# Layer 1's experts computed by columns, with a block's expert copied to a fixed tile, and whole batches stored at once

## The chip, the cores and the metric

The kernel runs on one core of a Trainium2 chip. The metric is the device time of one launch in microseconds, measured as the median of several runs. A profiled execution gives, beside its own time, a trace of every instruction on TensorE (PE, with its weight loads PEld), VectorE (DVE), ScalarE (ACT), GpSimd (POOL) and SyncE (SP).

## The reference

Four layers act on x [4, 256, 256] (batch, tokens, features) with a context [4, 512, 128], all in fp32. Each layer adds a cross-attention of the normalised x to x, and then a feed-forward of the normalised x:

```python
x = x + L0_xattn(ln(x), ctx);  x = x + L0_ffn(ln(x))   # routed low-rank adapters
x = x + L1_xattn(ln(x), ctx);  x = x + L1_ffn(ln(x))   # mixture of experts
x = x + L2_xattn(ln(x), ctx);  x = x + L2_ffn(ln(x))   # one of two experts
x = x + L3_xattn(ln(x), ctx);  x = x + L3_ffn(ln(x))   # 64 chosen tokens a batch

def L1_ffn(h):                      # E = 8 experts, top 2, F = 176, FS = 352
    scores = softmax(h @ gate.T)
    w, idx = top_k(scores, 2);  w = w / (sum(w) + 1e-20)
    cw = scatter(w, idx)                                # [tokens, E]
    g = silu(einsum('th,efh->tef', h, w_gate)) * einsum('th,efh->tef', h, w_up)
    y = einsum('te,teh->th', cw, einsum('tef,ehf->teh', g, w_down))
    return y + swiglu(h, sw_gate, sw_up, sw_down)       # the shared expert, FS wide
```

The layers 1 to 3 have 16 heads of 128 in their cross-attention, and this is where most of the time goes. The change is in `L1_ffn` and in how x is loaded at the beginning and stored at the end.

## The kernel before

The main function is `bounded_path`. x stays in SBUF for the whole kernel, one tile `x_sb[b]` of [128, 2, 256] for each batch: 128 partitions, two chunks of 128 tokens, 256 features. Behind `bounded_path` a register `again` is loaded from a word `over`, and a second, general path would run if it were set (it is not). That is line 2856 for the load and line 2859 for the branch, and each of the five engines does both.

The order of instructions on PE, ACT, DVE and POOL is the order in which the program writes them (`tc.manual_schedule`), so an instruction that waits holds up everything that its engine has after it. SP's order, with most of the loads and stores, is left to the framework. PSUM banks come from `bank(tag, ...)`: tag `s` has four, `mm` two, `o` and `t` one each. A tile with `bufs=n` is reused after n allocations. A matmul of fp32 appears in the trace as two records.

**Layer 1's FFN** lies between 583.9 and 709.4 us, and has two kinds of matmul work that are woven together.

*The shared expert* is class `Shared`, one object for each of 8 chunks of 128 tokens (two a batch). `rise` has the tokens as stationary operand and the weights (352 columns of `wgu`) as moving one: 4 matmuls, 8 records, into two `s` banks (L2131). ACT takes silu of one (L2136), DVE multiplies by the other (L2137). The result has tokens on partitions, so `turn` transposes it in three pieces (L2143), and ACT copies these to SBUF (L2145, L2146). `fall` has three matmuls with the down weights into the `o` bank (L2152), and DVE adds that bank to x (L2156).

*The routed experts* are class `Block`: 23 blocks of 128 slots. A slot holds one token of one expert, and a block belongs to one expert only. `gather` fetches the 128 tokens by an indirect DMA from POOL (L2267). `turn_in` transposes them (pxg, L2275), and ACT copies them to `xgT`. `rise` loads the number of the block's expert from `ebi` into a register of PE (L2281), multiplies the tokens by a slice of `wgu` that the register addresses, 2 × 176 columns (pgu, L2287), then silu on ACT (L2292), and on DVE the product with the slot's weight `wslot` (L2294). `turn` transposes that product in two pieces (pgT, L2300, L2301), and DVE copies them to `gT` (L2303, L2304). `fall` multiplies with the expert's down weights, 128 rows and then 48 rows of it (pyr, L2309, L2312), into the `o` bank; ACT copies the bank to `yr` (L2316), and SP writes it to `yd` in DRAM. Later class `Back` gathers from `yd` the two rows of each token, and DVE adds them to x.

Between these two stands the routing. `chosen` works out the two experts of each token (on DVE and ACT). `ranks`, `lists`, `listed` and `indices` work out which token goes to which slot, with long chains of small DVE operations; `ranks` has six matmuls on PE ahead of its chain (L2166 to L2168), and `listed` has 32 records on PE (plist, L2236) that take what DVE makes in L2235. The order, written out by hand, is

```python
ranks(); shared[2].turn(); shared[3].rise(); shared[2].fall(); lists()
shared[3].turn(); shared[4].rise(); listed(range(2 * N8)); indices(); shared[3].fall()
```

Then the blocks run as a pipeline of four steps: in turn j the loop does `turn_in` of block j + 2, `rise` of block j + 1, `turn` of block j and `fall` of block j − 1. Four gathers are issued ahead. After the loop the next layer's weights are folded (pm, L985, and n_sb, L1004) between the last two chunks of the shared expert.

The weights of this FFN are loaded during layer 1's attention of batch 0: `load_waiting` issues one waiting DMA for each of eight pairs of heads.

**The end.** `put` (L2769) adds the chosen tokens' FFN output to x: one matmul for each batch and chunk (L2775), a DVE addition (L2777), and a store of 128 tokens, 128 KB (L2781), on SP or on ACT's queue. `x` is loaded and stored with token c × 128 + p at partition p, chunk c, so a run of one partition is 1 KB.

## Time and profile before

| | |
|---|---|
| three runs | 1482.56, 1485.49, 1488.65 us (median 1485.49) |
| profiled execution | 1485.29 us, of which the span of its trace is 1483.6 us |
| granted TensorE clock | 0.993 of full, mean over the span |
| layer 1's FFN | 583.9 to 709.4 us |
| its blocks, first pxg to last pyr | 618.9 to 684.6 us |
| POOL's gathers of the blocks (L2267) | 23, 22.0 us busy |
| the DVE chain of `ranks` | 597.7 to 601.0 us |
| register load of `ebi` on PE (L2281) | 23, 0.30 us each |
| last two stores issued by SP and by ACT | 1474.5 to 1476.6 us, 1475.0 to 1476.6 us |

Busy times are by engine and count an instruction from its start to its end; for PE the ends are modelled, and consecutive matmuls overlap, so PE's pace is read from the starts or from the chain of waits. A trace comes from one execution. The chain of waits is the work that ended last, followed back from the last instruction.

### The profile page before, as it was taken

To read this page: it belongs to the slowest core of one execution; us is meant where nothing else is said; L and a number is where in the kernel's file an instruction comes from. 1 tells how busy PE (TensorE), PEld (TensorE's weight loads), DVE (VectorE), ACT (ScalarE), POOL (GpSimd) and SP (SyncE) were. 2 spreads that over 40 slices of the span, in tenths; PEclk is the share of its full clock that TensorE was granted. 3 is DMA by queue.
4 is the path that set the end of the run, shared out by engine and by line. 5 is a ranking of instruction groups with operands and counts; after the bars stand their busy time and mean duration, and the time that the engine had idled before them with its cause. 6 is when DMAs were issued, how large, how long until landed. Compare 5 with 4: busy or idle time off the path is not lost.

```text
span 1483.6 us, 19771 instructions
## 1 busy us (share of the span) xinstructions
PE 1442.5 (97%) x7311; PEld 937.3 (63%) x7311; DVE 898.1 (61%) x1946; ACT 573.2 (39%) x1100; POOL 665.4 (45%) x779
## 2 busy tenths in 40 slices
PE   8999999999999999999999999999999999999997
PEld 7665667566556666656556666666885566666666
DVE  5666783575676566423675656547345666767684
ACT  4666453433433333234443333333224433333331
POOL 2221332566665454231466655556003665455560
PEclk9999999999999999999999999999999999999998
DMA  5000210210000001271210000000311000000000
GB/s 164 2 1 2 67 50 26 74 35 0 8 1 8 1 8 47 58 215 48 61 32 8 8 1 1 1 1 0 107 36 44 18 0 1 1 0 1 1 1 31
DMA packets 40037, 43.36 MB, mean 29 GB/s; under 512 B 3898, under 2 KB 36891, under 8 KB 39933
## 3 DMA queue, kind: packets, MB, share of 16 engines
q1 hardware_dynamic: 36956, 35.85, 8.0%
q0 software_dynamic: 1872, 5.11, 1.3%
q8 instruction: 60, 0.98, 0.3%
q10 hardware_dynamic: 1104, 1.05, 0.2%
q14 instruction: 45, 0.36, 0.1%
HBM read 36.89 MB, written 5.11 MB: 28 GB/s over the span
## 4 chain that ended last, share of the span: by engine, by line
PE 88%; DVE 6%; POOL 4%; issue 2%; ACT 0%; DMA 0%; DVEq 0%; POOLq 0%; ACTq 0%
PE ps L1815 21%; PE po L1821 21%; PE paq L1785 5%; PE pao L1785 4%; PE pbq L1785 4%; PE pbo L1785 3%; PE ph L2492 2%; PE po L2529 2%; PE pgu L2287 2%; PE ps L1321 2%; PE po L1331 2%; PE pyf L1448 2%; PE paf L1398 1%; PE py L1897 1%; PE pm L985 1%
## 5 line engine op out<-in xcount | busy, mean ns | idle before, releaser
L1828 POOL TENSOR_TENSOR half<-pT 128x1024 f32<-128x1024 f32 x96 | 225.8, 2353 | 376.7 <-ACT pT L1818 326.9
L1815 PE MATMUL ps<-qT,cT 128*128 128x512 f32 x768 | 345.5, 592 | 0.0
L1821 PE MATMUL po<-pT,c_sb 128*128 128x512 f32 x768 | 345.2, 592 | 0.0
L1818 ACT ACTIVATE pT<-ps,mbias 128x512 f32<-128x512 f32 x384 | 263.6, 687 | 163.7 <-PE ps L1815 153.7
L1821 PEld LDWEIGHTS po<-pT,c_sb 128*128 128x128 f32 x768 | 145.9, 190 | 183.7 <-issue 183.7
L1815 PEld LDWEIGHTS ps<-qT,cT 128*128 128x128 f32 x768 | 138.8, 190 | 137.9 <-issue 137.3
L1825 ACT COPY oT<-po 128x512 f32<-128x512 f32 x96 | 56.2, 586 | 263.6 <-PE po L1821 263.6
L1862 POOL TENSOR_TENSOR oT<-oT,wide 128x512 f32<-128x512 f32 x90 | 116.2, 1311 | 26.2 <-DVE wide L1861 26.2
L1325 ACT ACTIVATE pT<-ps 128x512 f32<-128x512 f32 x128 | 66.1, 603 | 41.0 <-PE ps L1321 40.8
L1795 DVE TENSOR_TENSOR qT<-qT,paq 128x128 f32<-128x128 f32 x90 | 25.6, 284 | 89.8 <-ACT qT L1794 89.5
L1834 DVE TENSOR_TENSOR half<-half 128x512 f32<-128x512 f32 x96 | 72.1, 751 | 10.2 <-POOL half L1828 10.2
L1795 DVE TENSOR_TENSOR w<-w,pao 128x128 f32<-128x128 f32 x21 | 6.0, 286 | 109.4 <-ACT w L1794 109.4
L1836 DVE STREAM_TRANSPOSE turned<-half 128x512 f32<-128x512 f32 x96 | 68.3, 711 | 6.3
L1785 PEld LDWEIGHTS paq<-xnT_a,m_sb 128*128 128x128 f32 x360 | 58.0, 191 | 21.5 <-PE po L1821 10.5
L1785 PE MATMUL paq<-xnT_a,m_sb 128*128 128x128 f32 x360 | 70.7, 278 | 0.1
L1785 PE MATMUL paq<-xx,m_x 128*128 128x128 f32 x360 | 69.8, 276 | 0.0
L1840 DVE TENSOR_REDUCE sums<-turned 128x16 f32<-128x512 f32 x96 | 65.9, 686 | 3.3
L1785 PE MATMUL pao<-n_x,ox 128*128 128x128 f32 x336 | 65.2, 276 | 0.3 <-POOL ox L1711 0.3
L1861 DVE STREAM_TRANSPOSE wide<-rz 128x512 f32<-128x512 f32 x96 | 62.2, 686 | 0.1
L1794 ACT COPY qT<-paq 128x128 f32<-128x128 f32 x90 | 23.9, 265 | 85.2 <-PE paq L1785 82.8
L1798 DVE TENSOR_TENSOR qT<-qT,pbq 128x384 f32<-128x384 f32 x90 | 49.9, 554 | 9.4
L1785 PEld LDWEIGHTS paq<-xx,m_x 128*128 128x128 f32 x360 | 54.6, 192 | 0.0
(401 smaller groups left out, 2584.8 us busy)
## 6 DMA issues: line engine op xcount, KB each, us to landing
wo<-in_L_wo SPq DMA_DIRECT2D x12, 512.0 KB
wq<-in_L_wqT SPq DMA_DIRECT2D x11, 512.0 KB
yd<-yr SPq DMA_DIRECT2D x23, 128.0 KB
w<-in_F_w SPq DMA_DIRECT2D x4, 512.0 KB
wgu<-in_F_wgT SPq DMA_DIRECT2D x2, 880.0 KB
wgu<-in_F_wuT SPq DMA_DIRECT2D x2, 880.0 KB
wk<-in_L_wkT SPq DMA_DIRECT2D x11, 128.0 KB
wv<-in_L_wvT SPq DMA_DIRECT2D x11, 128.0 KB
```

The lines of the kernel that those rows point to most:

```text
L1325: nc.scalar.activation(pT[kp][:, j], ps[j], AF.Exp)
L1785: nc.tensor.matmul(p[:, at, :], lhsT=lhsT, rhs=rhs, start=(k == 0 and at == 0), stop=(k == len(of) - 1 and i == which[-1]),)
L1815: nc.tensor.matmul(ps, lhsT=cT[:, b, k * P : (k + 1) * P], rhs=qT, start=True, stop=True)
L1818: nc.scalar.activation(pT[:, k, :], ps, AF.Exp, bias=mbias[:, b, k : k + 1])
L1821: nc.tensor.matmul(po, lhsT=c_sb[:, b, k, :], rhs=pT[:, k], start=(k == 0), stop=(k == NK - 1))
L1825: done["head"] = nc.scalar.copy(raw, po).ins
L1828: nc.gpsimd.tensor_tensor(half, pT[:, 0:2], pT[:, 2:4], ALU.add)
L1834: nc.vector.tensor_tensor(part, half[:, 0], half[:, 1], ALU.add)
L1836: nc.vector.transpose(turned.rearrange("p f i -> p (f i)"), part)
L1840: nc.vector.tensor_reduce(sums[b, hp // 4][:, hp % 4, :], turned, AX.X, ALU.add)
L1861: nc.vector.transpose(wide, rzs[b, hp // 4][:, hp % 4, :, None].to_broadcast([P, NB, 32]))
L1862: eng.tensor_tensor(outs[b, hp], outs[b, hp], wide.rearrange("p f i -> p (f i)"), ALU.mult)
```

## The change

- The shared expert's object is now a whole batch. `rise(ks)` has the weights as stationary operand, 128, 128 and 96 columns of them, and 256 tokens as moving operand. The result has the hidden features on partitions and goes straight into `gT`; there is no `turn`. `fall(c)` is as before, for one chunk. The order around the routing is written anew.
- A block's expert is copied by DVE from `wr1`, a new tile of all experts' weights, to a fixed tile `we` (two buffers). The expert's number is loaded into a register of PE and of DVE. `rise` has `we` as stationary operand in three pieces (128 gate, 128 up, and 112 with the rest of both: 48 gate, 16 of zeros, 48 up), and the tokens as moving operand. Silu is in two pieces, the product also, and lands in `gT`; there is no `turn`. The slot's weight is applied by ACT on the way from the `o` bank to `yr`. The loop is one step shorter.
- `wr1` takes eight DMAs in place of four whole ones, `wgu` keeps the shared part, POOL zeroes the gap, and `load_waiting` issues two at a time.
- x has token 2p + c at partition p, chunk c: runs of 2 KB. `put` does its matmuls first, then the additions batch by batch, and stores each batch at once, 256 KB, odd ones on SP, even ones on ACT's queue. `put(0, [0])` stores nothing.
- `again` is loaded before the last `block` and `put`.

```diff
-        nc.sync.dma_start(x_sb[b], t["x"][b].rearrange("(c p) d -> p c d", p=P))
+        nc.sync.dma_start(x_sb[b], t["x"][b].rearrange("(p c) d -> p c d", c=NC))
...
+    FQ = 2 * P + 64 + FL
+    wr1 = load_fw("fa", [P, ND, NE, FQ], ...)
+    nc.gpsimd.memset(wr1[:, :, :, 2 * P + FL : 2 * P + 64], 0.0)
     wgu = load_fw(
-        "fa",
-        [P, 2, ND, FT],
+        "fs",
+        [P, 2, ND, FS],
...
-            load_waiting()
+            load_waiting(2)
...
+                def rise(self, ks):
+                    for k in ks:
                         m = min(P, FS - k * P)
+                        pp = bank("s", [P, 2, S], f"psh{self.b}_{k}")
+                        for i in range(2):
+                            for d in range(ND):
+                                nc.tensor.matmul(
+                                    pp[:m, i, :], lhsT=wgu[:, i, d, k * P : k * P + m],
+                                    rhs=xnT1[self.b][:, d, :],
+                                    start=(i == 0 and d == 0), stop=(i == 1 and d == ND - 1),
+                                )
+                        g = fp.tile([P, S], F32, tag="gs", name=f"gs{self.b}_{k}", bufs=3)
+                        nc.scalar.activation(g[:m], pp[:m, 0, :], AF.Silu)
+                        nc.vector.tensor_tensor(self.gT[:m, k, :], g[:m], pp[:m, 1, :], ALU.mult)
...
+                def weights(self):
+                    j = self.j
+                    self.e = nc.values_load(state["ebi"][0:1, j : j + 1], engines=[E.PE, E.DVE], ...)
+                    self.w = fp.tile([P, ND, FQ], F32, tag="we", name=f"we{j}")
+                    nc.vector.tensor_copy(self.w[:, :, None, :], wr1[:, :, bass.ds(self.e, 1), :])
+
                 def rise(self):
-                    e = self.e = nc.values_load(state["ebi"][0:1, j : j + 1], engines=[E.PE], ...)
-                    pp = bank("s", [P, 2, FE], f"pgu{j}")
-                    for d in range(ND):
-                        nc.tensor.matmul(
-                            pp, lhsT=self.xgT[:, d, :], rhs=wgu[:, :, d, bass.ds(e * FE, FE)],
-                            start=(d == 0), stop=(d == ND - 1),
-                        )
...
+                    pp = bank("s", [P, 3, P], f"pgu{j}")
+                    for k, m in enumerate((P, P, FQ - 2 * P)):
+                        for d in range(ND):
+                            nc.tensor.matmul(
+                                pp[:m, k, :], lhsT=self.w[:, d, k * P : k * P + m], rhs=self.xgT[:, d, :],
+                                start=(k == 0 and d == 0), stop=(k == 2 and d == ND - 1),
+                            )
+                    sg = fp.tile([P, 2, P], F32, tag="sg", name=f"sg{j}")
+                    nc.scalar.activation(sg[:, 0, :], pp[:, 0, :], AF.Silu)
+                    nc.scalar.activation(sg[64 : 64 + FL, 1, :], pp[:FL, 2, :], AF.Silu)
+                    self.gT = fp.tile([P, 2, P], F32, tag="gT", name=f"gT{j}")
+                    nc.vector.tensor_tensor(self.gT[:, 0, :], sg[:, 0, :], pp[:, 1, :], ALU.mult)
+                    nc.vector.tensor_tensor(
+                        self.gT[:FL, 1, :], sg[64 : 64 + FL, 1, :], pp[64 : 64 + FL, 2, :], ALU.mult
+                    )
...
-                    done["slots"] = nc.scalar.copy(yr, py).ins
+                    done["slots"] = nc.scalar.activation(yr, py, AF.Copy, scale=state["wslot"][:, j : j + 1]).ins
...
+            shared[0].fall(0)
             chosen(B - 1)
+            shared[1].rise([0, 1, 2])
             ranks()
+            shared[0].fall(1)
+            shared[1].fall(0)
+            shared.append(Shared(2))
+            shared[2].rise([0])
             lists()
+            shared[2].rise([1])
+            shared[1].fall(1)
             listed(range(2 * N8))
             indices()
+            shared[2].rise([2])
...
+            shared[2].fall(0)
+            shared[2].fall(1)
+            shared[3].rise([0])
-            for j in range(-2, NBLK + 2):
+            for j in range(-2, NBLK + 1):
...
+                    blocks[j + 2].weights()
                     blocks[j + 2].turn_in()
                 if 0 <= j + 1 < NBLK:
                     blocks[j + 1].rise()
                 if 0 <= j < NBLK:
-                    blocks[j].turn()
-                if 0 <= j - 1 < NBLK:
-                    blocks[j - 1].fall()
+                    blocks[j].fall()
...
+        ps = {}
         for c in chunks:
             for b in (2 * i + 1, 2 * i):
...
+        for b in (2 * i + 1, 2 * i):
+            for c in chunks:
+                xc = x_sb[b][:, c, cols]
+                nc.vector.scalar_tensor_tensor(xc, ps[b, c][:, cols], wts[:, b, c : c + 1], xc, ALU.mult, ALU.add)
+            if store:
+                (nc.sync if b % 2 else nc.scalar).dma_start(out[b].rearrange("(p c) d -> p c d", c=NC), x_sb[b])
...
+        again = nc.values_load(over[0:1, 0:1], ...)
         block(1, z)
         put(1, cols=z)
+    return again
```

## The prediction

> **What bounds the kernel now.** I read the page first: the totals and the shares of the chain that ended last.

> ```profile
> span 1483.6 us, 19771 instructions
> ...
> PE 1442.5 (97%) x7311; PEld 937.3 (63%) x7311; DVE 898.1 (61%) x1946; ACT 573.2 (39%) x1100; POOL 665.4 (45%) x779
> ...
> PE 88%; DVE 6%; POOL 4%; issue 2%; ACT 0%; DMA 0%; DVEq 0%; POOLq 0%; ACTq 0%
> ```

> TensorE is busy 97% of the span: an edit pays if it takes time from PE's stream or from PE's waits. So I read the stage of layer 1's FFN, 583.9 to 709.4 us, first by windows (columns: stretch, length, busy time of PE, PEld, DVE, ACT, POOL, granted clock, DMA share, GB/s), with the one half-clock stretch inside it:

> ```profile
> 583.90:709.40 125.50, 121.42 (x548) 79.62 (x546) 47.74 (x171) 49.60 (x137) 31.18 (x33) 0.99 0.38 112
> 609.00:612.50 3.50, 3.50 (x12) 2.85 (x12) 1.18 (x7) 0.00 (x0) 1.39 (x2) 0.51 0.00 0
> ```

> PE idles 4.1 us in 125.5; DVE works 48. Then the chain of waits in the stage (start, duration, what): it gives PE's pace by matmul width.

> ```profile
> 593.45 1.30 PE pysh L2152 x6
> 594.75 0.34 PE pgsT L2143 x3
> 598.06 2.37 PE psh L2131 x8
> ...
> 655.75 0.37 PE pxg L2275 x2
> 656.12 1.19 PE pgu L2287 x4
> 657.31 0.11 PE pgT L2300
> 657.42 0.11 PE pgT L2301
> 657.53 0.43 PE pyr L2309 x2
> 657.96 0.63 PE pyr L2312 x2
> ...
> 707.81 0.89 PE pm L985 x8
> ```

> A record (an fp32 matmul is two) costs 0.296 us at 352 columns (2.37/8), 0.217 at 256 (1.30/6), 0.111 at 128 (0.89/8). The middle six lines are one block: 2.84 us, back to back.

> **The change, part by part.** *Blocks.* PE loses the two transposes (0.22), and pgu goes from 1.19 to 12 records of 128 columns, 12 × 0.111 = 1.33. pxg and pyr keep their instructions: 0.37 + 1.33 + 1.06 = 2.76, so −0.08 a block, −1.8 for 23.

> *Shared expert.* Before, 8 chunks × (2.37 + 0.34 + 1.30) = 32.1. After, 4 batches × (24 records × 0.217 + 2 × 1.30) = 31.2: −0.9.

> *What the blocks add beside PE.* DVE loses the weighting (L2294, 0.40) and both copies, gains two mults of the copies' shapes, a register load and the weight copy of 128x736. Rows by form (line, busy, mean ns, idle before), then register loads and one SBUF-to-SBUF operation by line (min/median/max ns):

> ```profile
> L2303 DVE COPY gT<-pgT 128x128 f32<-128x128 f32 x23 | 6.5, 284 | 0.5 <-PE pgT L2301 0.5
> L1004 DVE COPY n_sb<-pn 128x512 f32<-128x512 f32 x8 | 5.4, 689 | 8.2 <-PE pn L1001 5.2 <-PE pm L985 3.0
> L2856 DVEq TENSOR_LOAD <-over x1: 542/542/542, 1474.4 to 1474.4; - x1
> L925 DVE TENSOR_SCALAR xn_f<-x_sb,mv_f,rstd_f x24: 404/1355/2166, 135.5 to 1046.0; 128x256 f32<-128x256 f32 x24
> ```

> From 284 at 128 elements to 689 at 512 is 1.05 ns an element: 736 make 0.92 us. Load, copy, mults: 0.54 + 0.92 + 0.55 = 2.0 us of DVE against 2.76 of PE: hidden, with 0.75 to spare. The dependence closes too: pgu's end, silu and mults, next copy, next pgu come to about 4 us, and the two buffers allow two blocks, 5.5. ACT has a second silu, 1.3 us a block; the slot weight rides on yr's copy. The register load on PE stays; POOL's gathers stay. Cost 0 with that cover. Without it, each 0.1 us a block beyond 2.76 is 2.3 us.

> The unknown is a DVE copy between SBUF tiles while POOL works. L925 is such a form: 0.40 us when it runs freely, 1.36 in the median, 2.17 at worst. Bounds for ours: 0.4 (it moves 2.9 times as much, so no less) and 0.92 + 1.8 (the worst hold-up) = 2.7. POOL's gather takes 0.96 us of each 2.8 (22.0 us for 23), so a copy meets one about a third of the time, and waits at most its length: 0.92 to 1.4 on average, and I take 0.92, nearest to the plain copies.

> [...]

> *The hand-written order and its waits.* What falls away or comes is read off the order of each engine. Before's idle is 4.1 us, or 4.8 with the 0.16 us by which each of some five waits is under-counted (a transpose is drawn 0.27 long and followed after 0.11). After, worked through with the rows' durations:
> - shared[1].fall(0) stands right behind shared[0].fall(1). Both use the single bank `o`. The add that frees it is queued on DVE behind ranks(), fourteen instructions and 3.3 us from prank on (597.7 to 601.0). PE ends the first fall at 599.1, the add ends at 602.2: 3.1 us idle. Everything on PE waits behind it.
> - The mult of shared[2].rise([0]) is on DVE ahead of lists(), so plist starts near 609.9: 1.6 idle, in place of 1.3.
> - fall(2,0) waits for its last mult (0.7), fall(2,1) for the add before it (0.7); the first pxg and the first pgu wait for xgT and the copy (0.6 + 0.5); fall(0,0) 0.2.
> - The loop is a step shorter: its tail has one wait for `o`, 0.6, where before had two.

> Sum 8.0. Stage: −1.8 − 0.9 + 8.0 − 4.8 = +0.5. Letting each wait end as early as its data allow gives −0.1. I take +0.3. The yd rows (SP) are read by Back's gathers with over 4 us in hand, and lose 2 of that: 0.

> *Clock.* The half-clock stretch cost 1.6 us. It follows a 1.26 us wait at 604.4; the other three of the kernel's body follow waits of 1.0, 1.7 and 2.5 us, while five waits of 1.1 to 1.9 us were followed by none. After has the same wait and a longer one: 0 to +1.7, I take +0.8. [...]

> *Loads.* 15 weight loads in place of 8 in layer 1's first batch, two per step, needed 260 us later: 0. x in runs of 2 KB instead of 1 KB: 0 to −0.3, taken −0.1.

> *End.* The last pieces, in the order of time and by line:

> ```profile
> 1474.09 1.13 DVE L2777 SCALAR_TENSOR_TENSOR x_sb<-py,wts,x_sb 128x128 f32<-128x128 f32 x4 [0.58 <-PE py L2775]
> 1474.47 2.14 SPq L2781 DMA_DIRECT2D out<-x_sb  x2
> ...
> L2859 SPq EVENT_SEMAPHORE  x8: 17/17/17, 1481.0 to 1481.5; - x8
> ...
> L2859 SPq COMPARE_BRANCH  x1: 45/45/45, 1477.3 to 1477.3; - x1
> ```

> SP issues two stores until 1476.6, loads `over` (0.53), branches, and goes on 3.7 us later, at 1481.0; then the end. After, SP has one store, after the second add (1474.7): issued by 1475.1, branch at 1475.7, on at 1479.4. ACT branches as early. The stores' data were in by 1478, so the branch still sets the end: −1.6, less 0.1 for a larger store. Bounds −0.2 (the store's 256 KB or another engine ends last) and −2.2 (the second store's long issue, 1.72, gone on both queues).

> **Sum**, against the profiled execution, 1485.29 us (span 1483.6 and 1.7 around it; the median of the runs, 1485.49, is 0.2 away): 1485.3 + 0.3 + 0.8 − 0.1 − 1.5 = **1484.8**. With the bounds of wait, clock and end: 1482 to 1488. Half a per cent, 7.4 us, is about what a measurement of this kernel can tell from no change; I forecast no change by that measure, 0.65.

> **Rivals.** *The copy paces the loop* (slower). Place: DVE's load, copy and mults, 23 times. It decides once load and copy pass 2.2 us (2.76 − 0.55). At 1.9 + 0.6 a block costs 3.05, +6.6 in all, less what the head of the loop hides: +5. At 2.7 + 0.54 it is 3.8, +24. Half held up, half not, lies between: 1490 to 1502, say 1494. [...] Against: POOL is busy 31 us of the stage's 125. Chance 0.18.

> *The small costs of the block's joints vanish* (faster). pxg takes 0.37 for 0.22 of transposes, and pyr 1.06 for 4 × 0.217 = 0.87: 0.34 a block that I keep, as it goes with the 48-row weights. If the register operations or the addressed operand pgu<-wgu cause it, 23 × 0.34 = 7.8 goes. With the bank wait partly filled and no second half clock (−0.8): 1485.3 − 7.8 − 1.5 + 0.3 = 1476.3, and 1474 to 1478. For: both stand beside addressed operands. Against: pyr's operand stays addressed. Chance 0.17.

> *The end does not move:* another engine's branch or the larger stores set it. 1486.1; inside my forecast.

> **How the numbers follow.** My own case 0.65, copy 0.18, joints 0.17. The range cuts the copy's upper part and the joints' lower: 1477 to 1491. Faster by over 0.5% is below 1478.1: the joints, 0.17. Slower, above 1492.9, is most of the copy's case and a little of mine with long waits: 0.17. The rest 0.66.

> **What would show it.** Right: a block of 2.7 to 2.8 us with pgu x12 near 1.33, the copy `we` near 0.9 us with PE never waiting for it, an idle of about 3 us at pysh behind ranks, the semaphores of the last branch near 1479.4. Wrong: PE waiting for `we` in every block; blocks below 2.5 us; a longer transfer in the last microseconds; more than two half-clock stretches in the stage.

## The result, and the profile after

The changed kernel is slower by a little: 1490.14 us median over 22 runs against 1487.30 for 22 runs of the kernel before, a ratio of 1.0019 (95% interval 1.0004 to 1.0035), so +2.8 us with 0.6 to 5.2. Its profiled execution took 1487.51 us, with a span of 1485.7.

The parts of the prediction can be read one by one. First the chain of waits of the changed kernel in the FFN stage (start, duration, what):

```profile
599.48 0.29 DVE ws L2215
599.77 0.34 DVE x_sb L2168
600.11 0.04 issue
600.15 2.93 PE pysh L2163 x6
603.08 3.35 PE psh L2150 x8
...
611.03 5.20 PE plist L2248 x32
616.23 3.50 PE psh L2150 x8
...
631.59 0.37 PE pxg L2287 x2
631.96 1.33 PE pgu L2306 x12
633.29 0.43 PE pyr L2322 x2
633.72 0.63 PE pyr L2325 x2
```

The block takes 0.37 + 1.33 + 0.43 + 0.63 = 2.76 us, as worked out. The wait for the bank is there too: ws ends the chain of ranks(), the add of the first fall follows, and only then the second fall starts. But look at that fall: six records take 2.93 us, where six took 1.30 before; eight records of 256 columns take 3.35, where the pace gives 1.74. PE runs at half clock here (0.50 granted). The windows of the same kernel show how often (stretch, length, busy PE, PEld, DVE, ACT, POOL, granted clock, DMA share, GB/s):

```profile
582.50:713.80 131.30, 123.38 (x694) 95.05 (x692) 56.17 (x175) 52.09 (x148) 32.08 (x33) 0.95 0.37 107
595.96:599.38 3.42, 1.63 (x9) 1.12 (x8) 2.94 (x14) 0.14 (x1) 0.00 (x0) 1.00 0.00 0
599.38:606.20 6.82, 6.05 (x14) 4.88 (x15) 1.10 (x4) 0.00 (x0) 0.00 (x0) 0.50 0.00 0
609.62:613.03 3.41, 2.00 (x19) 2.04 (x19) 3.41 (x16) 0.00 (x0) 0.00 (x0) 1.00 0.00 0
613.03:619.86 6.83, 6.83 (x25) 5.73 (x25) 1.92 (x11) 0.10 (x1) 2.15 (x2) 0.50 0.07 21
```

PE's waits in the stage, the longest in all first (engine, line, what it waited for: us in all, times, longest), and the weight copy by tile (min/median/max ns, first and last start):

```profile
PE pysh L2163 <- DVE x_sb L2168: 3.1, 2, 2.6
PE plist L2248 <- DVE at L2247: 1.6, 1, 1.6
PE pgu L2306 <- DVE we L2298: 1.1, 1, 1.1
PE pn L1001 <- ACT m_sb L993: 0.7, 1, 0.7
PE pyr L2322 <- ACT yr L2329: 0.6, 1, 0.6
PE pxg L2287 <- ACT xgT L2289: 0.5, 1, 0.5
```
```profile
L2298 DVE COPY we<-wr x23: 544/544/545, 626.8 to 684.2; 128x736 f32 x23
```

PE waits for the copy once, at the head of the loop, and never again. And the end, by line:

```profile
L2866 SPq EVENT_SEMAPHORE  x8: 17/17/17, 1483.2 to 1483.7; - x8
...
L2866 ACTq COMPARE_BRANCH  x1: 54/54/54, 1480.0 to 1480.0; - x1
L2866 SPq COMPARE_BRANCH  x1: 45/45/45, 1480.1 to 1480.1; - x1
```

From the end of the last matmul to the end of the span were 9.3 us (1474.3 to 1483.6), now 7.1 (1478.7 to 1485.7).

### The profile page after: what moved, and what is told of

Same layout as the page of the kernel before. It is cut to its first block, busy times and chain, and to the rows that moved or that the text cites. A ratio compares the mean times of both kernels' runs of the same rounds, so it can differ in the third digit from the quotient of the medians.

```text
span 1485.7 us, 20081 instructions
## 1 busy us (share of the span) xinstructions
PE 1443.7 (97%) x7457; PEld 953.8 (64%) x7457; DVE 907.0 (61%) x1950; ACT 576.3 (39%) x1111; POOL 668.1 (45%) x780
## 4 chain that ended last, share of the span: by engine, by line
PE 88%; DVE 6%; POOL 3%; issue 1%; ACT 0%; DMA 0%; POOLq 0%; DVEq 0%; ACTq 0%
PE ps L1815 21%; PE po L1821 21%; PE paq L1785 5%; PE pao L1785 4%; PE pbq L1785 4%; PE pbo L1785 4%; PE pgu L2306 2%; PE ph L2497 2%; PE po L2534 2%; PE ps L1321 2%; PE pyf L1448 2%; PE po L1331 2%; PE paf L1398 1%; PE psh L2150 1%; PE py L1897 1%
## 5 line engine op out<-in xcount | busy, mean ns | idle before, releaser
L1834 DVE TENSOR_TENSOR half<-half 128x512 f32<-128x512 f32 x96 | 72.2, 752 | 10.2 <-POOL half L1828 10.2
```

The lines of the kernel that those rows point to most:

```text
L1834: nc.vector.tensor_tensor(part, half[:, 0], half[:, 1], ALU.add)
```

## The experiments

Every kernel was timed in rounds beside the kernel before on the same chip. The theory: the change's work and its end are what the sum says or a little better; what turned the sign is half clock, brought by PE's waits in the new order. The rivals: that the columns form costs PE more than the sum, or that the end costs. For each profile I also give three numbers: the length from the first psh to the last paq (layer 1's FFN, layer 2 and layer 3's attention, of which only the first differs between the kernels), the half-clock time in it, and the length less half of that, which is about what it would have taken at full clock: where PE also waited in such a step, as for 0.8 us in the one from 599.38 in the changed kernel, it takes away up to half of that wait too much. The table follows the experiments.

**The end alone.** The kernel before with the new layout of x, `put` and `again`.

```diff
-        put(0, [0])
+        put(0, [0], store=False)
...
+        again = nc.values_load(over[0:1, 0:1], ...)
         block(1, z)
         put(1, cols=z)
```

> The kernel before with only the layout of x, the stores of whole batches and the earlier load of `again`; layer 1's FFN as before. In the trace of the changed kernel the last matmul ends 7.0 us ahead of the span's end, before 9.3. Theory (the clock took the gain, the end gave 2.3 us): -2.3 us against before, with the FFN stage unchanged. Rival (the end gave nothing, larger stores cost what the earlier branch gives): 0 within 1 us.

Measured: ratio 0.9984 (0.9965 to 1.0003), −2.4 us with −5.2 to +0.4. Its tail is 7.1 us long. But the tail of the old end is not always 9.3: in the four profiles that have it it was 9.3, 9.1, 7.7 and 7.2, a mean of 8.3. All ten profiles with the new end have 7.0 to 7.1, so the profiles put the gain between 0.1 and 2.2, 1.2 on average; the runs alone do not exclude zero.

**The FFN alone.** The changed kernel with the old layout, `put` and `again`: the reverse of the first.

> The changed kernel with loads, stores and `again` as before: the FFN part alone. Theory: the FFN stage costs about 5 us more than before, nearly all of it at half clock in the two stretches behind the waits at 597.6 and 609.4 us: +5 us against before, 2 to 8 by the run. Rival (the end costs, the FFN is even): 0 to +1.

Measured: 1.0033 (1.0012 to 1.0053), +4.9 us (1.8 to 7.9). The two parts add up: −2.4 + 4.9 = +2.5 against the +2.8 of the whole. The FFN part is what costs, and its profile has 10.2 us of half clock in the stage.

**The wait filled.** Work in place of the wait, nothing else moved.

```diff
             shared[0].fall(1)
+            pfill = bank("mm", [P, P], "pfill")
+            for _ in range(11):
+                nc.tensor.matmul(pfill, lhsT=ident, rhs=ident, start=True, stop=True)
             shared[1].fall(0)
```

> The changed kernel with 11 extra matmuls of the identity (22 records of 128 columns, 2.4 us, their result unused) written between shared[0].fall(1) and shared[1].fall(0), where PE waits 2.56 us for the bank. Theory (a window of 3.4 us in which PE works less than about half brings half clock in the next): the wait stays as long but PE works, the half-clock stretch from 599 us goes, the later one at 613 can stay; the stage is 2 to 4 us shorter than in the changed kernel, the time 2 to 3 us below it. Rival (the half clock comes from the kind of work or from the wait's place, not from idling): the stretch stays, and the time is 0 to +0.5 us against the changed kernel.

Measured: 1.0000 (0.9981 to 1.0019) against before, 2.8 us below the changed kernel's ratio, as forecast; but the two intervals overlap, and the runs alone do not show that the extra work made it faster. The windows of its profile, at the place of the wait and behind plist (columns as above):

```profile
606.10:609.50 3.40, 3.40 (x27) 3.24 (x27) 2.83 (x14) 0.23 (x1) 0.00 (x0) 1.00 0.00 0
609.50:612.90 3.40, 3.30 (x19) 2.81 (x19) 1.21 (x4) 0.00 (x0) 0.00 (x0) 1.00 0.00 0
...
618.03:621.44 3.41, 3.17 (x29) 3.19 (x29) 3.04 (x16) 0.00 (x0) 0.00 (x0) 1.00 0.02 5
621.44:624.85 3.41, 3.41 (x12) 2.57 (x12) 1.04 (x6) 0.00 (x0) 1.20 (x1) 0.50 0.00 0
```

No half clock follows the filled wait. (The profiled execution itself is this kernel's longest, 1494.74 us, with 27 us of half clock ahead of the stage.) One step of it still follows plist, and there is something new in that row: the step ahead of it, 618.03 to 621.44, has PE busy for 3.17 of 3.41 us. Those are records of plist, 46 columns each.

**The order mended.** The falls and pyr go to the two mm banks, idle in this stage, and the lists come earlier.

```diff
-                    py = bank("o", [P, D], f"pysh{self.b}_{c}")
+                    py = bank("mm", [P, D], f"pysh{self.b}_{c}")
...
-                    py = bank("o", [P, D], f"pyr{j}")
+                    py = bank("mm", [P, D], f"pyr{j}")
...
             shared[1].fall(0)
+            lists()
             shared.append(Shared(2))
-            shared[2].rise([0])
-            lists()
-            shared[2].rise([1])
+            shared[2].rise([0, 1, 2])
             shared[1].fall(1)
             listed(range(2 * N8))
             indices()
-            shared[2].rise([2])
...
-            shared[3].rise([0])
+            shared[3].rise([0, 1])
...
```

> The changed kernel with the falls and pyr in the two mm banks, which nothing else in the stage uses, lists() ahead of all three pieces of shared[2].rise, and shared[3].rise([0, 1]) ahead of the loop. Theory: the wait of 2.56 us goes, that before plist falls below 0.7 us, both half-clock stretches go; the stage takes 120 to 122 us instead of 129 to 131; 1479 to 1482, 5 to 7 us below before. Rival (blocks by columns cost PE more than the sum says, the clock is a side show): at most 3 us below the changed kernel.

Measured: 0.9953 (0.9936 to 0.9970), −7.0 us against before and faster than both kernels: 1480.91 median. The wait of 2.6 is gone, that before plist is 0.8, and the stage takes 122.4 us, where it took 125.5 before and 131.3 in the changed kernel. The half clock did not go altogether, and the windows show why not:

```profile
582.70:705.10 122.40, 118.28 (x694) 91.53 (x692) 55.95 (x175) 51.97 (x148) 31.99 (x33) 0.99 0.40 115
606.57:609.98 3.41, 3.41 (x33) 3.41 (x32) 2.57 (x14) 0.00 (x0) 0.00 (x0) 1.00 0.02 5
609.98:613.39 3.41, 3.41 (x9) 2.73 (x9) 1.47 (x7) 0.00 (x0) 1.82 (x2) 0.50 0.07 17
```

PE does not idle for a moment from 606.57 to 609.98, and is given half clock behind it. This step is filled by plist. In the kernel before it is the same. The step that holds its wait of 1.26 us is followed by full clock, and the next one, filled by plist, by the half-clock stretch at 609:

```profile
602.26:605.67 3.41, 2.16 (x8) 1.09 (x7) 3.31 (x10) 0.88 (x3) 0.00 (x0) 1.00 0.00 0
605.67:609.08 3.41, 3.40 (x31) 3.41 (x31) 2.81 (x15) 0.00 (x0) 0.00 (x0) 1.00 0.00 0
```

**The blocks alone.** The changed kernel with class `Shared`, and the order of its calls, taken from the kernel before.

> The changed kernel with the shared expert as before (by tokens, with its transposes and its order of work) and the blocks by columns. PE has no wait behind ranks() then. Theory (the blocks' form gains what the sum says, the shared expert's new order lost it): -1.8 for 23 blocks, -1.0 for the shorter tail, +1.1 for the loop's first copy, -2.3 for the end: 4 us below before, with one half-clock stretch in the stage as before. Rival (the columns form of the blocks is what costs): above before less 2.3, so 1486 or more where before is 1488.

Measured: 0.9979 (0.9961 to 0.9997), −3.1 us. The blocks by columns are worth what the sum said; with the change's end they make a faster kernel. What costs is the shared expert's part. The mended kernel keeps that part's new form and changes its banks and its order, and gains: so it is the order, with the bank that it shares.

**The waits elsewhere filled**, in the kernel before, the changed and the mended one. A filler writes what the first real matmul overwrites, as here:

```diff
         pt = bank("t", [P, ND, S], f"pxn_{name}")
+        for _ in range({"a0_1": 10, "f0_0": 4}.get(name, 0)):
+            nc.tensor.matmul(pt[:, 0, :P], lhsT=ident, rhs=ident, start=True, stop=True)
```

> The kernel before with matmuls of the identity, their results unused, written into PE's waits: 10 ahead of pxn of the second batch (a wait of 2.5 us near 28 us), 4 and 6 ahead of pT (52 and 87 us), 4 ahead of pxn at 135, 7 ahead of py at 168, 8 ahead of pz at 571, 6 ahead of plist. The work and the waits' ends stay. Theory (waits bring half clock in the next window, by luck of where the window falls): no half-clock stretch but the first, the median 4 us below before, and the runs lie within 5 us instead of 11. Rival (the half clock has another cause): 0 to +1 us, the same spread.

> The changed kernel with the same matmuls in the same waits, 11 in the wait for the bank behind ranks(), 7 ahead of plist and 4 ahead of the first pgu. Theory: without half clock the change is worth its work and its end alone: stage +0.5 to +0.7, end -2.3, so 1.6 us below the filled kernel before. Rival (the columns form costs more than the sum says): level with it or above.

> The mended order (falls and pyr in the two mm banks, lists() ahead of the three pieces) with the same matmuls in the waits outside the stage, 3 ahead of plist and 4 ahead of the first pgu. Theory: 3 to 5 us below the mended kernel, 1475 to 1478, and runs within 4 us. Rival: as the mended kernel, 1481.

Measured: 0.9965 (0.9950 to 0.9981), 0.9964 (0.9948 to 0.9979) and 0.9945 (0.9924 to 0.9966) against before. Useless matmuls make the kernel before 5 us faster, and its runs lie between 1479.2 and 1486.6 instead of 1482.9 and 1493.9 (12 runs beside 29), a wider band than the 5 us that I expected. The fillers at 52 and 87 us missed: they wait for the same bank as the matmul behind them, and run after the wait. The changed kernel comes out level with the kernel before once both are filled, where I expected it 1.6 us below; the interval of 2 us does not tell these apart. The changed kernel, filled, is 8 us below the changed kernel as it stands (1.0004 to 1.0035), clear of both intervals. The mended kernel gained less than expected (0.9945 beside 0.9953, within the intervals), and its profile shows 6.8 us of half clock behind plist.

**plist split.** Eight matmuls of the shared expert between the halves of plist; their DVE product is held back.

```diff
-            shared[2].rise([0, 1, 2])
+            shared[2].rise([0, 1])
             shared[1].fall(1)
-            listed(range(2 * N8))
+            listed(range(N8))
+            held = []
+            shared[2].rise([2], held)
+            listed(range(N8, 2 * N8))
+            nc.vector.tensor_tensor(*held[0])
...
```

> The mended kernel with the eight matmuls of shared[2].rise([2]) (1.7 us) between the two halves of plist, their DVE product behind the second half. plist has 46 columns a record; in seven profiles a window of 3.4 us filled by it was followed by half clock with PE hardly idle, and one in which it lay across two windows was not. Theory (a thin stream of columns counts as little as idling): no window is filled by plist, the half-clock stretch near 610 us goes, 0.5 to 2 us below the mended kernel, whose profile has one such stretch. Rival (only waits count): the stretch stays, the time within 0.5 us.

Measured: 0.9962 (0.9947 to 0.9977), 1478.96 median, no different from the mended kernel. The stretch behind 610 is gone, but one stands at 606.6 to 610.0: the step before it holds the wait of 0.85 us and the first half of plist:

```profile
603.22:606.63 3.41, 2.56 (x21) 2.16 (x20) 3.41 (x16) 0.00 (x0) 0.00 (x0) 1.00 0.00 0
```

That is what the theory would say of such a step, but it was said afterwards. The seven profiles of the expectation are six: before, wait filled, mended, blocks alone, changed filled and mended filled each have a full-clock step with 26 or more records of plist and half clock behind it. In before filled, plist lies across two steps, both busy for 3.41 us, and full clock follows.

**The loop's head.** The split kernel with two copies earlier, and the fillers.

```diff
+            for j in range(2):
+                blocks[j].weights()
             shared[2].fall(0)
             shared[2].fall(1)
-            shared[3].rise([0, 1])
+            shared[3].rise([0])
...
```

> The split kernel with the first two weight copies ahead of shared[2].fall(0), shared[3].rise([1]) between the first and the second pxg, and the matmuls of the identity in the waits outside the stage (28, 135, 168 and 571 us; those at 52 and 87 us wait for the same bank and run behind the wait). Theory: the waits of 0.5 and 1.1 us at the loop's head fall to 0.3 together, the clock losses outside go: 2 to 4 us below the split kernel, some 1475 to 1477. Rival (the head's waits come from the gathers' latency): the head's waits stay, 1 to 2 us below from the clock alone.

Measured: 0.9957 (0.9942 to 0.9971), 1480.61 median, where I expected 1475 to 1477: a miss. The waits at the head are gone, but the chain of waits shows a new one:

```profile
612.55 0.18 DVE ebi L2281
612.73 1.10 issue
613.83 4.30 PE pysh L2176 x11
```

`weights` also loads the expert's number into PE's register. Moved ahead of the falls, that load (at 612.9 in the trace) waits for `ebi`, and the falls wait behind it: 2.3 us. I had moved the copy and forgotten the instruction that it takes along.

**plist made dense.** The right operand is read three times over, so a record has 138 columns; the 32 take 4.01 us, where the thin ones of the mended kernel take 3.74.

```diff
-                        state["plist"], lhsT=at, rhs=state["bring"][:, i, c], ...
+                        state["plist"], lhsT=at, rhs=state["bring"][:, i, c][:, None].to_broadcast([P, 3, 2, NBLK]), ...
...
```

> The mended kernel with the right operand of plist's 16 matmuls read three times over, 138 columns a record instead of 46 (the second and third copy unused). At PE's pace 128 columns take the same 0.111 us as 46, so this adds 0.3 us in all and no wait. Theory (a stream of 46 columns counts as little as idling): no half-clock stretch right behind plist, though the mended kernel and the split one have one; 0.5 to 2 us below the mended kernel on average. Rival (only waits bring half clock): the stretch stays as often, the time 0.3 us above.

> The kernel before with the same threefold operand of plist and nothing else. It has a wait of 1.26 us just ahead of plist. Theory: no half clock behind plist, since the window with the wait still has 2 us of dense work; 1 to 3 us below before on average. Rival: the stretch stays, level with before.

Windows of the dense mended kernel, plist and what follows it:

```profile
607.20:611.21 4.01, 4.01 (x33) 4.01 (x34) 2.92 (x15) 0.00 (x0) 0.00 (x0) 1.00 0.02 4
611.21:615.00 3.79, 3.79 (x20) 3.31 (x19) 1.88 (x8) 0.00 (x0) 2.15 (x2) 1.00 0.12 35
```

And of the kernel before with a dense plist:

```profile
611.03:615.04 4.01, 4.01 (x33) 4.01 (x34) 2.92 (x15) 0.00 (x0) 0.00 (x0) 1.00 0.00 0
615.04:619.00 3.96, 3.96 (x19) 2.91 (x18) 1.46 (x7) 0.99 (x3) 2.17 (x3) 1.00 0.11 33
```

In both the clock stays full, behind waits as long as before (0.8 and 1.3 us). But the steps fall at other places than in the thin kernels, so one has to compare like steps. The dense mended kernel has one that matches the split kernel's at 603.22, with the same kind of wait and 16 records of plist in each:

```profile
605.70:609.11 3.41, 2.61 (x20) 2.21 (x19) 2.94 (x14) 0.00 (x0) 0.00 (x0) 1.00 0.00 0
609.11:612.53 3.42, 3.42 (x25) 3.26 (x25) 2.05 (x11) 0.00 (x0) 0.14 (x1) 1.00 0.02 5
```

With 2.56 us busy and thin records half clock followed; with 2.61 and dense ones it did not. In the dense kernel before, the step from 610.65 to 614.07 has 3.04 us busy, all of it plist; the step with 3.17 us of thin records in the kernel with the wait filled was followed by half clock.

The times do not settle it: 0.9955 (0.9936 to 0.9975) for the dense mended kernel, no better than 0.9953 for the mended one, where I expected 0.5 to 2 us; and 0.9986 (0.9968 to 1.0004) for the dense kernel before. The shortest run went from 1478.45 to 1477.10 and from 1482.64 to 1481.21, 1.4 us each, which is half of one half-clock step of 3.41 us less the 0.3 us that the columns cost. In the steps compared, half clock followed records of 46 columns and not those of 138, and two shortest runs fit that; the medians and ratios show it for neither kernel, and what makes the difference no run shows.

The table, one profile each, in us. "At full clock" takes half of the half-clock time away.

| kernel | first psh to last paq | half clock in it | at full clock |
|---|---|---|---|
| before | 837.8 | 3.4 | 836.1 |
| end alone | 839.4 | 6.8 | 836.0 |
| before, filled | 836.0 | 0 | 836.0 |
| before, dense plist | 836.3 | 0 | 836.3 |
| changed | 843.6 | 13.7 | 836.8 |
| FFN alone | 842.4 | 10.2 | 837.2 |
| changed, wait filled | 840.7 | 6.8 | 837.3 |
| changed, filled | 839.1 | 3.4 | 837.4 |
| blocks alone | 837.4 | 6.8 | 834.0 |
| mended | 834.8 | 3.4 | 833.1 |
| mended, filled | 836.4 | 6.8 | 833.0 |
| split | 834.8 | 3.4 | 833.1 |
| split, head | 835.1 | 3.4 | 833.4 |
| mended, dense plist | 833.2 | 0 | 833.2 |

The last column is the cleanest reading of this case. Kernels that do the same work in the same order agree within 0.6 us, though their raw lengths differ by up to 4.5. By it the changed order costs 0.7 to 1.3 us, the blocks alone gain 2.1, and the mended order gains 3.

## Why the prediction was wrong, point by point

I forecast no change, 1484.8 against 1485.3; measured is a slowdown of 0.2%, small, within half a per cent, but an interval that leaves out no change. The step that failed is the term for the clock: +0.8 us was taken, with one more half-clock step as the worst case, and the profile shows 5.1.

- *Blocks.* Right: 2.76 us a block, PE never waits for the copy inside the loop. The copy took 0.544 us, not 0.92.
- *Order and waits.* Right in kind and nearly in size. Forecast were 3.1 at the bank, 1.6 at plist, 0.6 + 0.5 at the head and 0.6 in the tail; the trace has 2.6, 1.6, 0.5 + 1.1 and 0.6. The head is longer since the first register load on DVE takes 0.55 us ahead of the copy. Stage at full clock: +0.3 taken, about +0.7 in the profile.
- *Clock.* Here the step failed. I took +0.8 with bounds 0 to +1.7, one more step at most. The profile has 10.2 us more half clock in the stage, and half of that, 5.1 us, is lost by the table's estimate; in the runs, where its share varies, the FFN part costs 4.9, of which some 1 is work. (One profile is one draw: the old order has 3.4, 6.8 and 3.4 us of half clock in the stage in before, the end alone and the blocks alone, the new one 13.7 and 10.2 in the changed kernel and the FFN alone.) I had counted the waits that were followed by half clock, four of nine, and had read the 1.26 us ahead of the stretch at 609 as its cause. The step with that wait was followed by full clock; the one right before the stretch is filled by plist, whose 46-column records keep PE busy for 3.40 of its 3.41 us. And I had taken the loss as one step: in the changed kernel each of the two stretches is two steps long, 6.83 us; why, no run isolates. My sign for being wrong counted stretches, and so missed it.
- *What half clock followed.* In the changed kernel a step with 1.63 us of work, in the mended one a step of 46-column records, busy for 3.41 of its 3.41 us.
- *Loads.* −0.1 was taken from no row. The first use of x on DVE comes 0.5 us earlier (4.0 against 4.5 us), that on PE at 8.05 against 8.08: nothing that the time shows.
- *End.* −1.5 forecast, bounds −0.2 to −2.2; −2.2 between the two profiles shown, −1.2 on average over the profiles with the old end. Right in size. SP goes on 3.1 us after its branch (1480.1 to 1483.2), where it was 3.7, and the end still follows that; why the old end took from 7.2 to 9.3 us is open.
- *The copy paces the loop* (rival): refuted. The 23 copies took 544 to 545 ns each, though 19 of them overlapped one of POOL's gathers. POOL's 23 gathers took 22.9 us in place of 22.0, no matter where four are ahead. Nor did the register load stand alone in DVE's time, as the rival's sum had it: from the third on it took 0.30 to 0.31 us, of which 0.27 to 0.28 lay beside the first mult.
- *The joints vanish* (rival): refuted. pxg takes 0.37 and pyr 1.06 as before, so these costs do not go with the operand that was removed; what they go with no run shows.
- *Where the sum lost its sign.* Ahead of the stage the changed kernel's profile is 1.5 us early (583.9 against 582.5), mostly for a half-clock step at 138 us that before has and this one has not. Then the stage: +0.7 at full clock and +5.1 for the clock. Then the end, −2.2. Together +2.1, and the spans differ by 2.1. The step at 138 is luck; those in the stage belong to the change.

## What to carry to other kernels

A short wait of the busiest engine can cost more than its length: behind the wait of 2.6 us the changed kernel's profile has 6.8 us of half clock. Half clock does not follow every such wait (four of nine in the profile before by the prediction's count, and of these four one stood behind plist), so price it between the wait alone and the wait plus half of the one or two steps of 3.41 us behind it, and look at the stream ahead: in the mended kernel a step filled by 46-column records, with PE busy for all of it, was followed by half clock. When an order is written by hand, look for two users of one bank back to back, and for what the release of that bank is queued behind: here two idle banks, with the lists called earlier, took the changed kernel from 2.8 us above the kernel before to 7.0 below it. And when two profiles of a kernel differ by several us in stretches that did not change, compare them at full clock before explaining anything.

## What the runs showed of the hardware

- Half clock came in steps of 3.41 us, which lie differently to the work in each run: the same wait of 1.85 us near 570 us is followed by half clock in the changed kernel's profile, where it lies within one step, and not in that of before, where two steps share it (0.68 + 1.17 us). With five of the waits of the kernel before filled, the standard deviation of its runs went from 3.0 us (29 runs) to 2.3 (12 runs).
- How little work brings half clock is not shown as a limit on busy time: in before's profile the step from 134.62 to 138.03, busy for 2.17 of 3.41 us, was followed by half clock, and the one from 168.76 to 172.17, busy for 1.83, was not.
- Useless matmuls in waits made the unchanged kernel 0.35% faster.
- 138 columns in place of 46 took plist from 3.7 to 4.0 us, and full clock followed it in both profiles.
- A store of 128 KB took 0.33 to 0.39 us to issue on SP's queue, but the last of six took 1.72, 1.79, 1.85 and 0.39 us in the four profiles with the old end.
